# Layer 0 of a two-layer vision Mamba: one x_proj product per chunk for both scan directions, with the kinds of states chosen anew for each half image

## The chip, the core and the metric

The kernel is one program on one core of a Trainium2 chip. The time is device microseconds (us) of one execution. Its engines are named as in the profile: PE (TensorE matrix products), PEld (the loading of TensorE's weights), DVE (VectorE), ACT (ScalarE), POOL (GpSimd) and SP (SyncE, which here issues nearly all DMAs). All data is float32.

## What is computed

The input has 8 images of 48 x 48 positions and 192 channels. Two layers follow each other, each with a residual. The change is in layer 0 alone, whose core is a selective scan over 384 inner channels with 16 states each, run in four directions:

```
xs    = stack([rows, columns, flip(rows), flip(columns)])     # u in four orders, k = 0..3
x_dbl = einsum('bkdl,kcd->bkcl', xs, x_proj_w)                # 12 dt rows, 16 B rows, 16 C rows
dt    = softplus(dt_w @ x_dbl[:12] + dt_bias)
h     = exp(dt*A) * h + (dt*u) * B                            # per step, channel and state
y     = sum over states of h * C
```

Directions 2 and 3 read the same u as 0 and 1, backwards. So x_dbl of direction 2 at a position is another matrix times the same column of u as x_dbl of direction 0. After the scan the four directions are summed, normalised, gated and projected to 192 channels. Layer 1 has two stages of bidirectional Mamba over lines; it keeps its instructions.

## The kernel before

**Tiling.** An *item* is one image, one direction and one chunk of 384 positions (8 rows or columns of 48). An image has 4 x 6 = 24 items, layer 0 has 192, and they run in the order of image, direction, chunk; two neighbours form a *pair*. An item has 16 states, a state has 3 blocks of 128 channels: 48 *segments* of 128 x 384 for each item, 9216 in layer 0. I call items of directions 0 and 1 the forward half of an image and those of 2 and 3 the backward half.

**What a segment costs.** ACT computes `exp(dt*A)` (tile `a`, L515). PE puts `dt*u*B` into one of three PSUM tiles `b`, and DVE runs the scan over both (L1290), which starts from `carry` where the chunk isn't the first. POOL multiplies a state's three blocks by C (tile `g`, L703, one instruction for each state), with C fetched over all partitions from DRAM by a DMA (`cc`, L472). PE adds the product into PSUM (`y`, L720).

**Kinds of states.** How `dt*u*B` is made is written by hand as a letter for each of the 16 states, in `WAYS[0]` (two rows for even and odd items). With kinds `a` and `b` the transposed `dt*u` (`dtu`) is multiplied by B, position by position, and PE transposes the result back: three transposes for each segment (L645). The multiplication is three ACT instructions (`bT`, L553) or one POOL instruction (L543): POOL may take a state only if it is a `b`, ACT may take either, and the planner says which. With kind `m` a diagonal matrix of B is made (`db`: three small ACT instructions, L597, or one of POOL, L594), and PE multiplies `dtu` by it (L639); a float32 product of this kind passes through PE twice, a transpose once. Two further rows hold for the last image, where no next image is being prepared.

**The x_proj step** (`project`, L330). For each item PE multiplies u by `xp` (three products, L350), ACT or DVE copies 44 rows into `xd`, SP stores the B and C rows to DRAM (`bc`, L368), PE transposes `xd` (L380) and ACT or DVE copies the transposed rows into `bt`, which kinds `a`, `b` and `m` read. Then `softplus` multiplies `xd` by `dtw` (L414) and ACT applies the function (L419). The bias of dt is a row of ones in `xd` at row `ONE`.

**What sets the order.** Each engine runs its instructions in program order. That order comes from a planner in the kernel (`Plan.run`): every step is a `Need` with a due time (a segment number plus an offset from `ORDER[0]`), a cost on each engine that may do it, and the steps it needs; the planner simulates the engines and gives each one the step with the lowest due time among those that are ready. `near` is how long past the earliest ready step another one may begin and still be chosen. Two PSUM banks are shared by all small products. A step marked `exps` waits for the planner's leave while ACT's softplus table is loaded.

Of the kernel before, what the change touches and what calls it, by code (L numbers as in the profile page):

```python
# [26 lines left out]
N = 16  # L27
R = 12
E = R + 2 * N
ONE = 64  # L30
RT = 8
T = RT * S
NC = L // T
# [4 lines left out]


WAYS = (  # L40
    ("aabbbbbabbbbbmab", "bbbbbbbabbbbbmab", "ambbmbbbbmbmabbm", "ababbbbmbbabbmba"),
    ("bbbbbbbbbbbdabbb", "bbbdbbbbbmbbabbb", "bbbbbbbbbbbdabbb", "bbbdbbbbbmbbabbb"),
)
PE, DVE, ACT, POOL, SP = "PE", "DVE", "ACT", "POOL", "SP"

# [16 lines left out]

ORDER = (
    dict(
        du=-40, turn=-31, fetch=4, exp=-4, weigh=-5, late_act=1.5, late_pool=1.5, matrix=-5, row=-2,
        wide=-7, there=8.5, zero=-0.5, multiply=-4, broad=-3.5, place=-8.5, carry=7.5, gather=1.5, add=6,
        leave=7, back=6, evac=-5, lo0=-40, mid0=-54, hi0=-42, lo1=-43, mid1=-43, hi1=-52, lead=0, apart=10,
        pro0=8, pro1=-140, pro2=220, tail0=3, tail1=6, near=0,
    ),
    dict(  # L70
        du=-16, turn=-13, fetch=-6, exp=-2, weigh=-3, late_act=1.5, late_pool=-2, matrix=-22.5, row=-24,
# [25 lines left out]
class Need(Mark):  # L97
# [2 lines left out]

    def __init__(self, due, costs, after=(), bank=False, frees=None, sets=(), lag=0.0, late={}, exps=False):
        Mark.__init__(self)
        self.exps = exps
        self.due, self.costs, self.after, self.wants = due, costs, list(after), bank
        self.late = late
        self.frees, self.sets, self.lag, self.bank = frees, sets, lag, None
# [14 lines left out]
class Plan:  # L123
# [4 lines left out]
    def __init__(self):  # L128
        self.clear = dict.fromkeys((PE, DVE, ACT, POOL, SP), 0.0)
        self.lanes = []  # L130
        self.banks = [Mark(0.0, PE), Mark(0.0, PE)]
        self.marks = {}
        self.at = -10**6
        self.exps = True
        self.near = 0.02

    def mark(self, *key):
# [21 lines left out]
        return need  # L159

    def ready(self, need, e):
        if need.exps and not self.exps:
            return None
        after = need.after
        while after and after[-1].t is None:
            return None
        t = 0.0
        for m in after:
            if m.t is None:
                after.remove(m)  # L170
                after.append(m)
                return None
            t = max(t, m.t + (0.0 if m.e == e else LAG[m.e][e]))
        if need.wants:
# [54 lines left out]
class Common:  # L229
# [100 lines left out]
    def project(self, plan, pool, p, pair, lo, mid, hi, which=(0, 1)):  # L330

        nc, mark = self.nc, plan.mark
        tiles = self.tiles.setdefault(p, {})
        gots = []
        for i in which:
            item = pair[i]  # L340
            g, wts = 2 * p + i, item["wts"]
            turned = item.get("turned")
# [11 lines left out]
            xd = self.xds[i]  # L354
            got = Need(at(), COPY, [n] + self.xd_used[i], frees=k)
            yield got
            if turned:
                self.copy(
                    got.e, xd[:E].rearrange("p (w h) -> p w h", h=S),
                    ps[:E, :T].rearrange("p (h w) -> p w h", w=RT),  # L360
                )
            else:
                self.copy(got.e, xd[:E], ps[:E, :T])

            def send(e, i=i, xd=xd):
# [3 lines left out]
                pair[i]["bc"] = tiles["bc"][i]  # L369

            after = [got] + ([mark("cc", g - 5, N - 1)] if g >= 6 else [])
            sent = Need(at(), {SP: 0.1}, after, lag=DMA, sets=[mark("bc", g)])
            yield sent
            send(SP)
            after = [got] + ([mark("place", (g - 2 - i) * NSEG - 1)] if g >= 4 else [])
            n = Need(at(), {PE: 0.33}, after, bank=True)
# [6 lines left out]
            n = Need(at(), {ACT: 0.16, DVE: 0.19}, [n], frees=k, sets=[mark("bt", g)])  # L383
            yield n
            if i == 0:
                tiles["bt"] = pool.tile([P, 2, TB, E], F32, tag="bt", name="bt", bufs=2)
            bt = tiles["bt"]
            item["bt"] = bt[:, i]
            self.copy(n.e, bt[:, i], ps[:, :T].rearrange("p (b e) -> p b e", e=P)[:, :, :E])
            self.xd_used[i] = [n, sent]  # L390
            gots.append(got)
        return gots

    def softplus(self, plan, pool, p, pair, due, after, which=(0, 1)):
# [29 lines left out]
        return ends  # L424

    def opens(self, plan, due, after, opened):
        yield Need(due, {ACT: TABLE}, after, sets=[opened])
        plan.exps = False

    def closes(self, plan):  # L430
# [44 lines left out]
    def stream(self, plan, pool, items, ways, decay, scan, finish, held, kept, weighed, fetched, first=None):  # L475
# [12 lines left out]
        total = len(items) * NSEG  # L488
        das, bts, ccs, bps, hs, gs = {}, {}, {}, {}, {}, {}
        self.xd_used, self.tiles = [[], []], {}  # L490
        way = lambda i, n: ways[2 * (i >= len(items) - 4 * NC) + i % 2][n]
        having = self.having = lambda i, some: [n for n in range(N) if way(i, n) in some]
        K = self.order

# [295 lines left out]
def layer0(ctx, cm, x, xs, x2, w, norm):  # L790
# [355 lines left out]
    def tails():  # L1146
# [4 lines left out]
        for b in range(NIMG):  # L1151
            st = None
            for c in range(NC - 1, -1, -1):
# [19 lines left out]
                for j in range(NJ):  # L1173
                    n = Need(at(), {ACT: 0.42}, [ready] + used[-1:])
                    yield n
                    sq = pool.tile([P, T], F32, tag="sq", name="sq", bufs=1)
                    nc.scalar.activation(sq, a[:, j, :], AF.Square)
                    n = Need(at(), {PE: MM}, [n], bank=(j == 0))
                    yield n
                    used.append(n)  # L1180
                    if j == 0:
                        ps, k = cm.bank(n, "var_ps"), n.bank
                    nc.tensor.matmul(ps[:, :T], ones, sq, start=(j == 0), stop=(j == NJ - 1))
                n = Need(at(), {ACT: 0.9}, [n], exps=True)
                yield n
# [2 lines left out]
                nc.scalar.activation(rs, rs, AF.Exp, scale=-0.5)  # L1188
                n = Need(at(), {DVE: 1.35}, [n], frees=k)
                yield n  # L1190
                nc.vector.tensor_tensor(a, a, rs.unsqueeze(1).to_broadcast((P, NJ, T)), ALU.mult)
                for j in range(NJ):
                    n = Need(at(), {ACT: 0.6}, [n])
# [67 lines left out]
    items, ys = [], {}  # L1261
    for b in range(NIMG):
        for k in range(4):
            rev = k >= 2
            order = range(NC - 1, -1, -1) if rev else range(NC)
            for n, c in enumerate(order):
                item = dict(
                    b=b, k=k, c=c, reverse=rev, carried=(n > 0), A=A[:, k],
                    wts=dict(xp=xp[:, k], dtw=dtw[:, k, :]),
                    u=lambda j, k=k, c=c: by_rows(seen(u, j, k, c), k), turned=k % 2,  # L1270
                    all=seen(u, slice(None), k, c),
                    ready=ready(b, k, c),
                    cost=(MM, 3.1 if k % 2 else 2.6, 0.915),
                    wanted=lambda j, b=b, k=k, c=c: wanted(b, k, c),
                )
                item["softened"] = [mark("dt", len(items))]
                if k < 2:
# [43 lines left out]
def layer1(ctx, cm, x2, xw, dst, w, norm):  # L1321
# [230 lines left out]
    def output(p):  # L1552
# [39 lines left out]
        nc.sync.dma_start((dst if stage else xw)[b][:, :, cs], o)  # L1592

    items = [
        dict(cost=(MM, 2.6, 0.855), sooner=0 if i else SOON, wanted=lambda j, i=i: [mark("silu z", i)]) for i in range(2 * pairs)
    ]

    def first(ps):
# [22 lines left out]
def laid_out(a):  # L1621
# [31 lines left out]
    t["w0_xp"] = widened(np.moveaxis(inner(g("x_proj_w")), 2, 3))  # L1653
# [37 lines left out]
```

## Time and profile before

| | us |
|---|---|
| three runs | 19351.8, 19359.31, 19360.32 (median 19359.31) |
| the profiled execution | 19360.51 |
| its span, which the trace covers | 19358.8 |
| layer 0 in the span (to the first instruction of layer 1) | 0 to about 9704 |

Cut at the first scan of each half image, layer 0 falls into halves of 718.6 and 622.0 us for image 0, of 584.6 to 588.8 (forward) and 608.9 to 614.6 (backward) for images 1 to 6, and of 563.8 and 582.9 for image 7.

The page counts an engine as busy while it runs an instruction, and neighbours on ACT and PE overlap: the mean duration of one is longer than its pitch, the time from its start to the start of the next. Costs are therefore taken from pitches. The timeline prints runs of equal instructions with a start, a length and a number, from which a pitch can be read. The view of stretches gives the busy time of each engine between two times.

### The profile page before, as it was taken

Reading aid. Unit: us, or ns where it says so; the run is one execution under the profiler, and the core shown is the slowest. Engines: PE = TensorE matmul, PEld = TensorE weight load, DVE = VectorE, ACT = ScalarE, POOL = GpSimd, SP = SyncE. Lnnn points to the kernel's source line nnn. Section 1 sums busy time; section 2 is a strip of 40 time slices with the busy share of each in tenths; the row PEclk is TensorE's granted clock in tenths of the full one; section 3 lists DMA queues with packets and bytes.
Section 4 is the critical chain, followed back from the end, with each engine's and each line's share of the span. In section 5 each row is a group of like instructions: output and inputs, shape, how many; then the busy total and the mean of one; then the engine's idle time right before and its main releaser. Section 6 shows DMA issues by size and latency. Waiting matters only on the chain.

```text
span 19358.8 us, 400059 instructions
## 1 busy us (share of the span) xinstructions
PE 18941.4 (98%) x137182; PEld 15944.7 (82%) x137182; DVE 18648.0 (96%) x23348; ACT 19012.3 (98%) x37123; POOL 18799.2 (97%) x8817
## 2 busy tenths in 40 slices
PE   9999999999999999999999999999999999999999
PEld 7888888888888888888878888888888888888887
DVE  8999999999999999999989999999999999999999
ACT  8999999999999999999999999999999999999999
POOL 7999999999999999999989999999999999999999
PEclk9999999999999999999999999999999999999999
DMA  3333333333333333333322222222222222222222
GB/s 91 95 104 95 98 103 94 106 93 99 100 93 108 92 106 97 91 96 85 90 70 72 71 72 70 71 71 71 71 76 72 74 74 74 74 75 74 74 74 71
DMA packets 1572608, 1640.56 MB, mean 85 GB/s; under 512 B 602000, under 2 KB 1536144, under 8 KB 1570448
## 3 DMA queue, kind: packets, MB, share of 16 engines
q1 hardware_dynamic: 1560592, 1588.75, 30.0%
q8 instruction: 1093, 17.91, 0.4%
q10 hardware_dynamic: 9984, 26.21, 0.4%
q14 instruction: 939, 7.69, 0.1%
HBM read 1439.32 MB, written 171.05 MB: 83 GB/s over the span
## 4 chain that ended last, share of the span: by engine, by line
PE 39%; ACT 6%; DVE 3%; issue 1%; POOL 1%; DMA 0%; POOLq 0%; DVEq 0%; ACTq 0%; SPq 0%
PE y L720 12%; PE b L645 11%; PE o_ps L1575 3%; PE xi_ps L1423 3%; PE z_ps L1477 3%; ACT l_da L515 2%; DVE h L1536 2%; ACT bT L553 2%; PE dt_ps L414 2%; PE xd_ps L350 1%; POOL g L703 1%; PE b L639 1%; PE du_ps L457 1%; PE yb_ps L778 1%; PE bb_ps L659 0%
## 5 line engine op out<-in xcount | busy, mean ns | idle before, releaser
L703 POOL TENSOR_TENSOR g<-h,cc 128x1152 f32<-128x1152 f32 x6144 | 14127.6, 2339 | 366.7 <-DVE h L1290 79.4
L645 PE MATMUL b<-ident,bT 128*128 128x128 f32 x50436 | 7997.3, 274 | 146.1 <-DVE h L1290 92.7
L1536 DVE TENSOR_TENSOR_SCAN h<-l_da,b 128x384 f32<-128x384 f32 x9216 | 8061.0, 932 | 67.8 <-PE b L645 44.1
L720 PE MATMUL y<-ident,g 128*128 128x128 f32 x55296 | 7995.4, 273 | 110.3 <-POOL g L703 88.0
L645 PEld LDWEIGHTS b<-ident,bT 128*128 128x128 f32 x50436 | 6079.7, 141 | 2124.3 <-issue 991.1
L1290 DVE TENSOR_TENSOR_SCAN h<-a,carry,b 128x384 f32<-128x384 f32 x7680 | 7081.0, 991 | 296.5 <-ACT a L515 147.7
L553 ACT ACTIVATE bT<-dtu,bt 128x384 f32<-128x384 f32 x11949 | 6941.3, 613 | 10.5 <-PE b L645 8.2
L720 PEld LDWEIGHTS y<-ident,g 128*128 128x128 f32 x55296 | 6403.4, 141 | 482.4 <-POOL g L703 234.6
L515 ACT ACTIVATE a<-dt,l_A 128x384 f32<-128x384 f32 x9216 | 5180.4, 611 | 60.6 <-DVE h L1290 45.3
L515 ACT ACTIVATE l_da<-dt,l_A 128x376 f32<-128x376 f32 x9216 | 5045.0, 605 | 15.9 <-DVE h L1536 12.8
L543 POOL TENSOR_TENSOR bT<-dtu,bt 128x1152 f32<-128x1152 f32 x1621 | 3450.6, 2130 | 57.8 <-PE b L645 37.1
L1290 DVE TENSOR_TENSOR_SCAN h<-a,b 128x384 f32<-128x384 f32 x1536 | 1340.7, 934 | 38.9 <-PE b L645 14.2
L446 POOL TENSOR_TENSOR du<-dt,u 128x1152 f32<-128x1152 f32 x384 | 1082.0, 2818 | 79.6 <-ACT dt L419 79.6
L966 PE MATMUL cv_ps<-pad,diag 128*128 128x384 f32 x2376 | 950.7, 487 | 0.0
L414 PE MATMUL dt_ps<-xd,l_dtw 128*128 128x384 f32 x2304 | 899.2, 496 | 39.8 <-ACT dt L419 27.9
L1575 PE MATMUL o_ps<-z,l_out 128*96 128x384 f32 x2304 | 918.0, 486 | 0.4 <-DVE b L627 0.3
L1477 PE MATMUL z_ps<-xt,l_z 96*128 96x384 f32 x2304 | 916.5, 489 | 2.0 <-DVE u L1452 1.9
L1423 PE MATMUL xi_ps<-xt,l_u 96*128 96x384 f32 x2304 | 907.9, 490 | 9.5 <-ACT xt L1406 6.6
L350 PE MATMUL xd_ps<-u,l_xp 128*128 128x384 f32 x2304 | 895.5, 487 | 1.9 <-ACT bt L273 0.7
L639 PE MATMUL b<-db,dtu 128*128 128x128 f32 x6264 | 829.4, 277 | 5.7 <-DVE h L1290 2.3
L639 PEld LDWEIGHTS b<-db,dtu 128*128 128x128 f32 x6264 | 772.5, 192 | 53.4 <-DVE h L1290 7.5
L1452 DVE SCALAR_TENSOR_TENSOR u<-xi_ps,l_conv_w,u 128x376 f32<-128x376 f32 (+1 forms) x1152 | 665.9, 581 | 24.9 <-ACT u L1442 17.8
(132 smaller groups left out, 12673.8 us busy)
## 6 DMA issues: line engine op xcount, KB each, us to landing
cc<-bc SPq DMA_DIRECT2D x6144, 192.0 KB, 3.1
y<-yt SPq DMA_DIRECT2D x96, 576.0 KB, 3.4
yo<-y SPq DMA_DIRECT2D x96, 576.0 KB, 4.1
xc<-in_x SPq DMA_DIRECT2D x174, 288.0 KB, 4.2
carry<-h SPq DMA_DIRECT2D x2560, 1.5 KB, 2.3
z<-v SPq DMA_DIRECT2D x144, 192.0 KB, 3.3
z<-z SPq DMA_DIRECT2D x48, 576.0 KB, 5.2
v<-v SPq DMA_DIRECT2D x126, 192.0 KB, 2.7
```

The lines of the kernel that those rows point to most:

```text
L515: nc.scalar.activation(dst, src, AF.Exp, scale=item["A"][:, j, n : n + 1])
L543: nc.gpsimd.tensor_tensor(to, of, by.to_broadcast((P, TB, DI)), ALU.mult)
L553: nc.scalar.activation(to[:, b, :], of[:, b, :], AF.Copy, scale=by[:, b, :])
L639: nc.tensor.matmul(ps[:, b * P : (b + 1) * P], item["dtu"][:, b, j * P : (j + 1) * P], dbs[i, n][:, b, :], start=True, stop=True,)
L645: nc.tensor.transpose(ps[:, b * P : (b + 1) * P], of, self.ident)
L703: nc.gpsimd.tensor_tensor(to.rearrange("p j t -> p t j"), h, c, ALU.mult)
L720: nc.tensor.matmul(item["sum"][b][:, j * P : (j + 1) * P], gs[f][:, j, b * P : (b + 1) * P], self.ident, is_transpose=True, skip_group_che ...
L1290: nc.vector.tensor_tensor_scan(order(h[:, :, at % NJ]), order(a), order(b), carry[:, at : at + 1] if item["carried"] else 0.0, ALU.mult, A ...
L1423: nc.tensor.matmul(pieces(ps), wu[d][0][:, m, j * P : (j + 1) * P], lines(xt, m, d), start=(m == 0), stop=(m == NM - 1),)
L1477: nc.tensor.matmul(pieces(ps), wz[d][0][:, m, j * P : (j + 1) * P], lines(xts[p % 3], m, d), start=(m == 0), stop=(m == NM - 1),)
L1536: nc.vector.tensor_tensor_scan(h[:, :, at % NJ], a, b, 0.0, ALU.mult, ALU.add)
L1575: nc.tensor.matmul(ps[:CP, :T], wout[:, 2 * stage + e, j, m * CP : (m + 1) * CP], items[2 * p + e]["z"][:, j, :], start=(e == 0 and j == 0 ...
```

## The change

It has four parts, all in layer 0 but for unused branches:

- `xp` holds for each of the two orders the rows of both directions, 88 in all. An item of directions 0 and 1 computes and copies all 88, transposes them, and stores them to DRAM twice: as they are (all 88 rows, `part`) and transposed (the backward direction's 44, `turn`).
- An item of directions 2 and 3 has no x_proj product, no copy and no transposes: SP loads its 12 dt rows into `xd` and its transposed rows into `bt`. Its C rows are fetched from the stored `part`. The row of ones moves from 64 to 96, so that 88 rows fit.
- `WAYS[0]` has three pairs of rows: forward, backward, last image. The forward rows are those of before; a backward row has three `m` where it had one, and the last image's rows are placed otherwise.
- In `ORDER[0]` some offsets differ (`mid0` -54 to -58, `carry` 7.5 to 6, `fetch` 4 to 3, `near` 0 to 0.02 and others), and two flags keep ACT's softplus table from being loaded between the tail's sum of squares and the exponential that needs it, and the reverse.

```diff
-ONE = 64
+ONE = 96
 WAYS = (
-    ("aabbbbbabbbbbmab", "bbbbbbbabbbbbmab", "ambbmbbbbmbmabbm", "ababbbbmbbabbmba"),
+    ("aabbbbbabbbbbmab", "bbbbbbbabbbbbmab", "abmbbbbabmbbbmab", "bmbbbbbabmbbbmab", "abmbmbbbbmbmbbam", "bbaabbbmbbabbmba"),
...
-        du=-40, turn=-31, fetch=4, exp=-4, weigh=-5, late_act=1.5, late_pool=1.5, matrix=-5, row=-2,
-        wide=-7, there=8.5, zero=-0.5, multiply=-4, broad=-3.5, place=-8.5, carry=7.5, gather=1.5, add=6,
-        leave=7, back=6, evac=-5, lo0=-40, mid0=-54, hi0=-42, lo1=-43, mid1=-43, hi1=-52, lead=0, apart=10,
-        pro0=8, pro1=-140, pro2=220, tail0=3, tail1=6, near=0,
+        du=-40, turn=-31, fetch=3, exp=-4, weigh=-5, late_act=1.5, late_pool=1.5, matrix=-5, row=-4,
+        wide=-6, there=8, zero=-2, multiply=-4, broad=-6.5, place=-8.5, carry=6, gather=1.5, add=6,
+        leave=7, back=6, evac=-4, lo0=-40, mid0=-58, hi0=-42, lo1=-45, mid1=-41, hi1=-52, lead=0, apart=10,
+        pro0=8, pro1=-140, pro2=210, tail0=3, tail1=6, near=0.02,
...
# project(), for each item of a pair
+            bt = tiles["bt"][:, i]
+            item["bt"] = bt[:, :, :E]
+            free = [mark("place", (g - 2 - i) * NSEG - 1)] if g >= 4 else []
+            if "other" in item:
+                got = Need(lo, {SP: 0.2}, self.xd_used[i] + free + [mark("kept", item["other"])], lag=DMA, sets=[mark("bt", g), mark("bc", g)])
+                yield got
+                part, turn = item["saved"]
+                nc.sync.dma_start(xd[:R], part[E : E + R, :])
+                nc.sync.dma_start(bt[:, :, :E], turn)
+                item["bc"] = part[E + R : 2 * E, :]
+                self.xd_used[i] = []
+                gots.append(got)
+                continue
...
-                self.copy(got.e, xd[:E], ps[:E, :T])
+                self.copy(got.e, xd[:e], ps[:e, :T])
...
+            if "saved" in item:
+                part, turn = item["saved"]
+                nc.sync.dma_start(part, xd[:e, :])
+                item["bc"] = part[R:E, :]
...
+            cost = {ACT: 0.16, DVE: 0.19} if e == E else {ACT: 0.27, DVE: 0.33}
...
+            if "saved" in item:
+                n = Need(at(), {SP: 0.1}, [n, sent], lag=DMA, sets=[mark("kept", g)])
+                yield n
+                nc.sync.dma_start(turn, bt[:, :, E:])
# stream()
-        way = lambda i, n: ways[2 * (i >= len(items) - 4 * NC) + i % 2][n]
+        way = lambda i, n: ways[2 * items[i]["kind"] + i % 2][n]
# the two flags
+        if (need.exps and not self.exps) or (need.calm and self.fragile):
-        yield Need(due, {ACT: TABLE}, after, sets=[opened])
+        yield Need(due, {ACT: TABLE}, after, sets=[opened], calm=True)
-                    n = Need(at(), {PE: MM}, [n], bank=(j == 0))
+                    n = Need(at(), {PE: MM}, [n], bank=(j == 0), exps=(j == 0))
# layer0(), for each item
-                    wts=dict(xp=xp[:, k], dtw=dtw[:, k, :]),
+                    wts=dict(xp=xp[:, k % 2], dtw=dtw[:, k, :]), rows=2 * E, kind=2 if b == NIMG - 1 else k // 2,
+                if k < 2:
+                    part = cm.dram.tile([2 * E, T], F32, name=f"xd{b}_{k}_{c}")
+                    turn = cm.dram.tile([P, TB, E], F32, name=f"bt{b}_{k}_{c}")
+                    item["saved"] = saved[b, k, c] = part, turn
+                else:
+                    item["other"], item["saved"] = b * per + (k - 2) * NC + c, saved[b, k - 2, c]
```

More of the change, by code (lines that the diff above doesn't have):

```diff
@@ L40 @@
 WAYS = (
-    ("aabbbbbabbbbbmab", "bbbbbbbabbbbbmab", "ambbmbbbbmbmabbm", "ababbbbmbbabbmba"),
-    ("bbbbbbbbbbbdabbb", "bbbdbbbbbmbbabbb", "bbbbbbbbbbbdabbb", "bbbdbbbbbmbbabbb"),
+    ("aabbbbbabbbbbmab", "bbbbbbbabbbbbmab", "abmbbbbabmbbbmab", "bmbbbbbabmbbbmab", "abmbmbbbbmbmbbam", "bbaabbbmbbabbmba"),
+    ("bbbbbbbbbbbdabbb", "bbbdbbbbbmbbabbb"),
 )
@@ L97, with __init__ @@
 class Need(Mark):
-    def __init__(self, due, costs, after=(), bank=False, frees=None, sets=(), lag=0.0, late={}, exps=False):
+    def __init__(self, due, costs, after=(), bank=False, frees=None, sets=(), lag=0.0, late={}, exps=False, calm=False):
         Mark.__init__(self)
-        self.exps = exps
+        self.exps, self.calm = exps, calm
         self.due, self.costs, self.after, self.wants = due, costs, list(after), bank
@@ L133, in __init__ @@
         self.at = -10**6
-        self.exps = True
+        self.exps, self.fragile = True, 0
         self.near = 0.02
@@ L161, in ready @@
     def ready(self, need, e):
-        if need.exps and not self.exps:
+        if (need.exps and not self.exps) or (need.calm and self.fragile):
             return None
@@ L341, in project @@
             g, wts = 2 * p + i, item["wts"]
+            xd = self.xds[i]
+            if i == 0:
+                tiles["bt"] = pool.tile([P, 2, TB, item["rows"]], F32, tag="bt", name="bt", bufs=2)
+            bt = tiles["bt"][:, i]
[11 more added lines that the diff above has]
+                continue
             turned = item.get("turned")
@@ L353, in project @@
                 )
-            xd = self.xds[i]
+            e = item["rows"]
             got = Need(at(), COPY, [n] + self.xd_used[i], frees=k)
@@ L358, in project @@
                 self.copy(
-                    got.e, xd[:E].rearrange("p (w h) -> p w h", h=S),
-                    ps[:E, :T].rearrange("p (h w) -> p w h", w=RT),
-                )
-            else:
-                self.copy(got.e, xd[:E], ps[:E, :T])
-            def send(e, i=i, xd=xd):
+                    got.e, xd[:e].rearrange("p (w h) -> p w h", h=S),
+                    ps[:e, :T].rearrange("p (h w) -> p w h", w=RT),
+                )
+            else:
+                self.copy(got.e, xd[:e], ps[:e, :T])
+            after = [got]
+            if "saved" not in item:
+                after += [mark("cc", g - 5, N - 1)] if g >= 6 else []
+            sent = Need(at(), {SP: 0.1}, after, lag=DMA, sets=[mark("bc", g)])
+            yield sent
+            if "saved" in item:
[3 more added lines that the diff above has]
+            else:
                 if i == 0:
@@ L368, in send @@
                 nc.sync.dma_start(tiles["bc"][i], xd[R:E, :])
[L369 to L376, printed above, removed]
+                item["bc"] = tiles["bc"][i]
+            n = Need(at(), {PE: 0.33}, [got] + free, bank=True)
             yield n
@@ L382, in project @@
                 )
-            n = Need(at(), {ACT: 0.16, DVE: 0.19}, [n], frees=k, sets=[mark("bt", g)])
+            cost = {ACT: 0.16, DVE: 0.19} if e == E else {ACT: 0.27, DVE: 0.33}
+            n = Need(at(), cost, [n], frees=k, sets=[mark("bt", g)])
             yield n
[L385 to L389, printed above, removed]
+            self.copy(n.e, bt, ps[:, :T].rearrange("p (b e) -> p b e", e=P)[:, :, :e])
             self.xd_used[i] = [n, sent]
             gots.append(got)
+            if "saved" in item:
+                n = Need(at(), {SP: 0.1}, [n, sent], lag=DMA, sets=[mark("kept", g)])
+                yield n
+                nc.sync.dma_start(turn, bt[:, :, E:])
         return gots
@@ L1182, in tails @@
                         ps, k = cm.bank(n, "var_ps"), n.bank
+                        plan.fragile += 1
                     nc.tensor.matmul(ps[:, :T], ones, sq, start=(j == 0), stop=(j == NJ - 1))
@@ L1190, in tails @@
                 yield n
+                plan.fragile -= 1
                 nc.vector.tensor_tensor(a, a, rs.unsqueeze(1).to_broadcast((P, NJ, T)), ALU.mult)
@@ L1259, in put_carry @@
         nc.sync.dma_start(carry[:, q * NJ : (q + 1) * NJ], h[:, 0 if rev else T - 1, :])
-    items, ys = [], {}
+    items, ys, saved = [], {}, {}
     for b in range(NIMG):
@@ L1276, in layer0 @@
                 item["softened"] = [mark("dt", len(items))]
+                if k < 2:
+                    part = cm.dram.tile([2 * E, T], F32, name=f"xd{b}_{k}_{c}")
+                    turn = cm.dram.tile([P, TB, E], F32, name=f"bt{b}_{k}_{c}")
+                    item["saved"] = saved[b, k, c] = part, turn
+                else:
+                    item["other"], item["saved"] = b * per + (k - 2) * NC + c, saved[b, k - 2, c]
                 if k < 2:
@@ L1594, in layer1 @@
     items = [
-        dict(cost=(MM, 2.6, 0.855), sooner=0 if i else SOON, wanted=lambda j, i=i: [mark("silu z", i)]) for i in range(2 * pairs)
+        dict(cost=(MM, 2.6, 0.855), rows=E, kind=0, sooner=0 if i else SOON, wanted=lambda j, i=i: [mark("silu z", i)]) for i in range(2 * pairs)
     ]
@@ L1652, in laid_out @@
     t["w0_conv_b"] = inner(g("conv_b"))
-    t["w0_xp"] = widened(np.moveaxis(inner(g("x_proj_w")), 2, 3))
+    v = np.moveaxis(inner(g("x_proj_w")), 2, 3)
+    t["w0_xp"] = widened(np.concatenate([v[:, :2], v[:, 2:]], -1))
     t["w0_dtw"] = with_bias(g("dt_w"), g("dt_bias"))
```

## Prediction

> **What bounds layer 0.** The change touches layer 0 alone, so I first cut the span there and read the busy times of one image's two halves, forward and then backward (time; busy us and instructions of PE, PEld, DVE, ACT, POOL; clock, DMA share, GB/s).
>
> ```profile
> core 0: us, PE busy (x) PEld busy (x) DVE busy (x) ACT busy (x) POOL busy (x), PEclk, DMA share, GB/s
> 3732.00:4320.00 588.00, 576.08 (x4227) 490.52 (x4226) 553.56 (x646) 581.12 (x1147) 580.70 (x284) 1.00 0.34 95
> 4320.00:4930.00 610.00, 586.04 (x4334) 498.92 (x4333) 579.76 (x682) 602.93 (x1177) 589.47 (x285) 1.00 0.39 103
> ```
>
> ACT is busy 98.8% in both halves. POOL is level with it in the forward half and has 3% to spare in the backward one; DVE has 5 to 6%. The halves of the other images from 1 to 6 last as long within 5 us. In images 1 to 7 (1340 to 9673 us) ACT is busy 8236 of 8333 us: 97 us idle. The waits of that stretch say who waits for whom (us, times, longest):
>
> ```profile
> ACT pad L956 <- PE xi_ps L915: 23.6, 21, 4.0
> ACT v L280 <- PE xi_ps L915: 15.3, 17, 5.4
> ...
> DVE h L1290 <- ACT a L515: 133.0, 76, 5.1
> DVE h L1290 <- issue: 39.8, 59, 2.5
> DVE h L1290 <- PE b L645: 37.5, 92, 1.8
> ```
>
> DVE's largest wait is for ACT; ACT's own waits are small and spread. So ACT's work sets the pace, and a gain must be ACT time that goes away, or some of those 97 us.
>
> **Pitches.** Instructions overlap with the next, so I price by the time from start to start, from the timeline at 4400 us (start, length, what, how many):
>
> ```profile
> 4400.07 1.00 ACT L597 ACTIVATE db<-ident,bt 128x128 f32<-128x128 f32 x3
> ...
> 4400.95 2.15 ACT L515 ACTIVATE a<-dt,l_A 128x384 f32<-128x384 f32 x4
> ...
> 4405.34 0.74 PEld L639 LDWEIGHTS b<-db,dtu 128*128 128x128 f32 x6 [0.16 <-DVE h L1290]
> ...
> 4408.15 0.36 PEld L645 LDWEIGHTS b<-ident,bT 128*128 128x128 f32 x3
> ...
> 4419.65 1.23 ACT L273 COPY yt<-y 128x384 f32<-128x384 f32 x3
> ```
>
> One `a` lasts 0.61 us, so four in 2.15 have a pitch of (2.15 - 0.61)/3 = 0.51; `bT` has the same shape and gets 0.51. Three `db` take from 4400.07 to the next start at 4400.95: 0.88. A copy of 384 columns lasts 0.48, so (1.23 - 0.48)/2 = 0.37. On PE a pass of 128 columns takes 0.11 ((0.36 - 0.14)/2), a product of kind m two of them, and a pass of 384 columns 0.325 (starts of neighbouring `xd_ps` rows). On POOL a `bT` takes 2.07 and a `db` 0.80, on DVE a copy 0.46 (starts again).
>
> **The counts.** I set the instructions of both programs against each other, engine by engine. Outside layer 0's rows below nothing changes in number; table loads stay at 602.
>
> *ACT.* `bT` 11949 to 11670: -279 x 0.51 = -142.3. `db` 384 to 807: +423 x 0.293 = +123.9. `xd` copies 265 to 190 (width in time is 384 columns whether 44 or 88 rows): -75 x 0.37 = -27.8. `bt` copies of 132 columns 264 to 143: -121 x 0.15 (their start-to-start time) = -18.2; 57 new ones of 264 columns: the trace has none, so between 0.15 and 0.37, taken at 0.26, half way as their width is: +14.8 (bounds +8.6 and +21.1). Other copies and biased copies that the planner now gives to ACT: 16 x 0.37 + 15 x 0.46 = +12.8. Sum **-36.7 us**, bounds -43 to -30.
>
> *POOL.* `bT` -75 x 2.07 = -155.3, `db` +27 x 0.80 = +21.6: **-134**. *DVE.* Fewer copies: **-25**. *PE.* 288 x_proj products less: -288 x 0.65 = -187; 288 transposes less: -32; 1512 transposes become products: 1512 x 0.11 = +166: **-53**.
>
> So the shared product itself saves ACT little (copies, about -31 us); its point is the PE time, which pays for more `m` states, and those spare ACT 3 x 0.51 = 1.53 for 0.88.
>
> **Where it lies.** The same sums for each half image, cut at each engine's own 576th step:
>
> | us | ACT | POOL | DVE | PE |
> |---|---|---|---|---|
> | image 0 | +6.7 | -29.9 | -6.9 | -3.9 |
> | images 1 to 6, forward halves | +2.2 | +21.3 | -4.7 | -0.4 |
> | images 1 to 6, backward halves | -38.0 | -125.5 | -11.9 | -19.2 |
> | image 7 | -7.6 | +0.5 | -1.4 | -29.0 |
>
> In the backward halves ACT's saving (6.3 each) is on the path: ACT stays the fullest engine (604 of about 605, POOL 567, DVE 582, PE 567 in pitches). POOL's 21 us per half become idle time, worth nothing beyond ACT's. Forward halves: nothing. Image 0: its +7.5 on ACT falls into the first half, where ACT is idle 12%; I count 0 (bounds 0 and +7.5). Sum: +2.2 - 38.0 - 7.6 = -43.4. Against the profiled execution (19360.5): 19317; the median of the runs lies 1.2 lower, so **19316**, 0.22% less than before.
>
> **The moved and added waits.** Each backward item adds two loads on SP, each forward item one more store: 192 DMAs more among some 6,300 of layer 0, at 0.3 to 0.6 us of issue; SP needs about 0.8 us of issue in a state of 2.8. Nothing shows these loads; the nearest rows are the `xd` store (48 KB, median 2.3 us, 1.5 to 7.0) and the `y` load (576 KB, 4.1). They are due 40 segments, some 38 us, before their item, so they are hidden: 0. Without that cover, 48 pairs x 2.3 to 7.0 would cost 110 to 336; below nothing, the first `cc` fetch of a backward item need no longer wait for a fresh store, at most the 1.6 us that POOL waits for `cc` in the stretch. The load waits for `xd` and `bt` to be free; behind it on SP stand `cc` fetches and carries. A `cc` fetch runs up to four states (11 us) ahead of its use and lands in 3.2, so some 8 us of delay are free; a `carry` store is needed an item later. The two flags hold back a PE step or a table load in the planner; in the trace no softplus falls between a tail's first square sum and its exponential (48 of 48), so I count 0.
>
> Smaller pieces have a rule against them. The Trainium skill (DMA: Bandwidth & Descriptors, Specifications) asks for at least 512 bytes a piece and says that smaller ones are read, modified and written back. The transposed store and load go in pieces of 176 bytes. But the `carry` store goes in pieces of 4 bytes, and landed after 2.6 us in the median and 8.7 at most in one backward half. By the rule these loads would be slower, by the row they land within the 38 us; the sum is the same.
>
> **Where the order could take it back.** The planner made a new order with other offsets, so the 97 us of idle time are not kept by right; that is the main uncertainty. What the order itself shows is calm: in forward halves a segment is placed on PE 8.0 segments (mean) ahead of the additions, before it was 8.2; in backward halves 9.1 against 8.5. Image 7 of before already runs with some 43 `m` states in each half, and there ACT is busy 561.7 of 564 and 574.2 of 582: more `m` has not made ACT wait.
>
> **Rivals.**
>
> *The forward halves pay.* POOL's load rises 2 to 5 us in each forward half of images 1 to 6, by 21.3 in all, and POOL is as busy there as ACT. If POOL sets the pace there, 21 less 2 already counted goes: 19316 + 19 = **19335**. For: 580.7 of 588 busy. Against: part of it is only the cut, since one `du` step moves from the backward half across it, and POOL's backward half has room.
>
> *Idle time goes as well.* With POOL 5% emptier in backward halves and fewer small products on PE, ACT may wait less. Half of the 97 us: 19316 - 48 = **19268**. For: ACT's waits are for PE products. Against: PE's load in the forward halves, where most of those products lie, stays.
>
> *PE cannot place the `m` segments in time; slower.* A state of kind m needs 3 x (0.74 + 0.36) = 3.3 us of PE with its additions by the timeline, its three scans 3 x 0.93 = 2.8; three PSUM tiles allow two scans of lead. With 168 more such states, each stalled by s, the gain is gone at s = 43/168 = 0.26 us, and slower by over 0.2% needs 0.49. At 0.5 us: 19316 + 84 = **19400**. Against: the scans waited 4.6 us in all for the 228 such states of images 1 to 7, 0.02 each. For: in images 1 to 6 PE is fuller than in image 7. In passes it has 564 us of work in a forward half of 587 and 570 in a backward one of 610.
>
> How full PE is, the skill reads otherwise. It (Perfetto Trace Analysis, Identifying the Most-Contended Engine) discards PE's busy share and takes that of weight loading: 490.5 of 588 here, 83%. By the passes above it is 96%. By the rule this rival would have no chance and the sum would stand; by the rows it keeps one.
>
> *It does not do what it says.* Excluded by count: 1152 x_proj products become 864.
>
> **Numbers.** Chances: forecast (19298 to 19330) 0.46, forward halves pay or the idle time grows a little (19331 to 19380) 0.24, idle time goes as well 0.16, slower rival 0.14. About 0.2% (39 us) is what a measurement of this kernel can tell from no change: the marks are 19321 and 19398. Of the forecast's case some two thirds lie below 19321: 0.31, with 0.16 makes faster 0.47; slower takes 0.13 of the last rival; the rest, 0.40, is the same. The range leaves out the deepest part of the idle case and half of the slower one: 19262 to 19392.
>
> **What would show it.** Right: backward halves of images 1 to 6 last 603 to 607 us, forward ones 586 to 590; ACT stays at 98.5 to 99%; POOL falls to 94% in backward halves; no wait for the `bt` or `xd` loads; layer 1 within 3 us. Wrong: scans waiting for products of kind m well over 0.1 us for each such state, ACT below 98%, forward halves over 592, or layer 1 moved.

## The result, and the profile after

The changed kernel takes **19391.39 us** (median of 17 runs, 19380.89 to 19398.28), the kernel before 19355.75 in the same measurement (17 runs, 19347.9 to 19360.32): a ratio of 1.0018, 95% interval 1.0011 to 1.0024. It is 36 us slower; 43 us less were forecast. The profiled execution of after took 19380.89 (span 19379.2), at the low end of its runs, that of before 19360.51 (span 19358.8), at the high end. So the traces hold 20.4 of the 36 us, and the account by place below goes by spans.

Cut at the first scan of each half image, the difference of the two spans lies here:

| us | forecast | measured |
|---|---|---|
| image 0 | 0 | +12.4 |
| images 1 to 6, forward halves | +2.2 | +2.3 |
| images 1 to 6, backward halves | -38.0 | **+10.8** |
| image 7 | -7.6 | -4.5 |
| layer 1 | 0 | -0.6 |
| sum | -43.4 | +20.4 |

Of the 63.8 us between the two sums, 48.8 are in the backward halves of images 1 to 6 and 12.4 in image 0. The view of stretches for image 3's two halves in after (time; busy us and instructions of PE, PEld, DVE, ACT, POOL; clock, DMA share, GB/s), the halves that the prediction shows of before:

```profile
core 0: us, PE busy (x) PEld busy (x) DVE busy (x) ACT busy (x) POOL busy (x), PEclk, DMA share, GB/s
3754.80:4341.40 586.60, 574.91 (x4215) 487.30 (x4213) 550.38 (x642) 582.47 (x1149) 580.58 (x284) 1.00 0.37 98
4341.40:4952.60 611.20, 587.01 (x4459) 511.35 (x4460) 580.34 (x679) 595.19 (x1179) 573.63 (x279) 0.99 0.38 104
```

In the backward half ACT's busy time fell from 602.9 to 595.2 and POOL's from 589.5 to 573.6: the work left, as counted. The half still lasts 611 us. ACT is idle 16 us of it, where it was idle 7. Over images 1 to 6 as one stretch, first before and then after, the same view says:

```profile
1340.50:8526.70 7186.20, 6975.07 (x51382) 5940.57 (x51380) 6797.37 (x7953) 7099.41 (x13925) 7027.92 (x3402) 1.00 0.36 98
```

```profile
1353.00:8552.30 7199.30, 6979.13 (x52036) 5996.76 (x52034) 6780.48 (x7895) 7067.75 (x13959) 6925.38 (x3362) 1.00 0.38 100
```

ACT was spared 31.7 us (7099.4 to 7067.8; the count for these images was 35.8). Its **idle time grew from 86.8 to 131.6 us**, by 44.8. All of the growth is in the backward halves: summed over the six images, ACT's idle time goes from 49.2 to 103.3 us there, and from 37.6 to 28.2 in the forward halves. The view of waits of the stretch from 1340 to 9650 us names what ended that idle time in after (waiter, releaser; us, times, longest):

```profile
ACT a L535 <- DMA cc<-xd: 20.2, 2, 10.5
ACT a L535 <- DMA u<-v: 18.8, 2, 9.5
ACT a L535 <- DVE h L1318: 15.3, 29, 6.0
ACT yt L273 <- PE y L740: 14.9, 5, 5.8
...
ACT a L535 <- DMA carry<-h: 8.6, 1, 8.6
```

Three releasers here are DMAs, and their five waits last 47.6 us, some 9 us each. In before the same view has one such line:

```profile
ACT a L515 <- DMA carry<-h: 6.6, 1, 6.6
```

An exponential `a` doesn't read `u`, `cc` or the store of `carry`. So the name of the releaser is a label that needs a look: what stands ahead of that `a` in ACT's program order? The timeline of ACT at the end of image 3 in after, the kernel's own line L1107:

```profile
4869.37 0.53 ACTq L1107 DMA_DIRECT2D u<-v  x1
4869.50 0.60 ACT L573 ACTIVATE bT<-dtu,bt 128x384 f32<-128x384 f32 x1
4870.01 0.60 ACT L535 ACTIVATE a<-dt,l_A 128x384 f32<-128x384 f32 x1
4870.43 9.65 ACTq L1107 DMA_DIRECT2D u<-v  x2
4880.13 0.61 ACT L535 ACTIVATE a<-dt,l_A 128x384 f32<-128x384 f32 x1 [9.52 <-DMA u<-v]
```

and of before (L1087):

```profile
4840.47 0.53 ACTq L1087 DMA_DIRECT2D u<-v  x1
4841.04 0.84 ACTq L1087 DMA_DIRECT2D u<-v  x1
4841.30 0.64 ACT L515 ACTIVATE a<-dt,l_A 128x384 f32<-128x384 f32 x1
4841.91 0.63 ACTq L1087 DMA_DIRECT2D u<-v  x1
4843.02 0.60 ACT L515 ACTIVATE a<-dt,l_A 128x384 f32<-128x384 f32 x1
```

Here ACT itself issues DMAs: three loads of 1152 KB each that bring the next image's `u`, issued by `enters()` two items before the image begins. Before, all three go out within 1.5 us. After, the third goes out 9.1 us behind the second, and ACT stands behind it. The gaps ahead of the third load at the end of images 1 to 6 are 7.7, 8.3, 8.6, 9.0, 8.6 and 4.6 us: 46.9 in all, about the size of the new idle time. In before the same place costs 5.5 us, all of it at the end of image 6. A seventh gap, of 8.6 us, stands at the end of image 0 (3.1 in before).

**Why the third load waits.** Each DMA of layer 0 is counted by one of eight semaphores (100 to 107), taken in turn in program order. In every program here a DMA is issued only once the one eight places earlier, which holds its semaphore, has landed. The landing events of the trace, after (start of the issue, issuer, what, semaphore, us to the last landing):

```
4869.37 ACT u<-v      100   8.03
4870.43 ACT u<-v      103  10.32
4872.00 SP  carry<-h  106   7.49     <- landed at 4879.49
4872.56 SP  cc<-xd    107   8.38
4879.56 ACT u<-v      106   6.08
```

The three loads stand at places n, n+3 and n+6 of the order of DMAs; before they stood at n, n+3 and n+4. Semaphore 106 was last taken by a `carry` store that SP issued *after* the first two loads. That store is 1.5 KB and otherwise lands in 2 to 3 us; behind two large loads it took 7.5. So ACT waits for a small store that is slow behind ACT's own loads. At the end of image 0 the third load's semaphore is still held by the first load itself. Before, the third load's semaphore was last taken by a `carry` issued at 4836.47, which landed at 4840.83, ahead of the load.

### The profile page after: what moved, and what is told of

The parts are those of the page before. It is cut to its first block, busy times and chain, and to the rows that moved or that the text cites. A ratio compares the mean times of both kernels' runs of the same rounds, so it can differ in the third digit from the quotient of the medians.

```text
span 19379.2 us, 401618 instructions
## 1 busy us (share of the span) xinstructions
PE 18930.5 (98%) x137830; PEld 15998.6 (83%) x137830; DVE 18624.3 (96%) x23264; ACT 18980.6 (98%) x37159; POOL 18667.9 (96%) x8769
## 4 chain that ended last, share of the span: by engine, by line
PE 61%; ACT 17%; DVE 4%; POOL 2%; issue 2%; DMA 1%; DVEq 0%; POOLq 0%; SPq 0%; ACTq 0%
PE y L740 19%; PE b L665 18%; ACT a L535 6%; ACT bT L573 5%; PE o_ps L1603 3%; PE xi_ps L1451 3%; PE z_ps L1505 3%; PE b L659 3%; PE dt_ps L434 2%; PE cv_ps L986 2%; POOL g L723 2%; DVE h L1564 2%; PE xd_ps L366 2%; ACT l_da L535 2%; PE du_ps L477 1%
## 5 line engine op out<-in xcount | busy, mean ns | idle before, releaser
L665 PE MATMUL b<-ident,bT 128*128 128x128 f32 x48924 | 7759.8, 274 | 161.9 <-DVE h L1318 85.5
L665 PEld LDWEIGHTS b<-ident,bT 128*128 128x128 f32 x48924 | 5879.0, 141 | 2037.9 <-issue 917.3
L573 ACT ACTIVATE bT<-dtu,bt 128x384 f32<-128x384 f32 x11670 | 6786.0, 613 | 21.5 <-PE b L665 19.4
L563 POOL TENSOR_TENSOR bT<-dtu,bt 128x1152 f32<-128x1152 f32 x1546 | 3280.2, 2123 | 58.4 <-PE b L665 34.4
L659 PE MATMUL b<-db,dtu 128*128 128x128 f32 x9288 | 1239.1, 277 | 5.4 <-DVE h L1318 4.6
L659 PEld LDWEIGHTS b<-db,dtu 128*128 128x128 f32 x9288 | 1150.6, 192 | 77.2 <-DVE h L1318 12.0
L366 PE MATMUL xd_ps<-u,l_xp 128*128 128x384 f32 x1728 | 668.0, 487 | 0.9 <-issue 0.5
```

Source lines behind the costliest of these rows:

```text
L563: nc.gpsimd.tensor_tensor(to, of, by.to_broadcast((P, TB, DI)), ALU.mult)
L573: nc.scalar.activation(to[:, b, :], of[:, b, :], AF.Copy, scale=by[:, b, :])
L659: nc.tensor.matmul(ps[:, b * P : (b + 1) * P], item["dtu"][:, b, j * P : (j + 1) * P], dbs[i, n][:, b, :], start=True, stop=True,)
L665: nc.tensor.transpose(ps[:, b * P : (b + 1) * P], of, self.ident)
```

## The experiments

Two kinds of kernels were tried: those that alter the loads of `u`, and those that separate the four parts of the change.

**One large load instead of three**, in after and in before.

```diff
-                    for i in range(3):
-                        part = slice(i * L // 3, (i + 1) * L // 3)
-                        nc.scalar.dma_start(u[:, :, part], vs[b][:, :, part])
+                    nc.scalar.dma_start(u, vs[b])
```

> The changed kernel with one edit: ACT fetches the next image's u with one DMA where it issued three. Theory A (the third of the three loads must wait for a small transfer of SP that stands behind the first two, and ACT waits with it, 4.6 to 9.5 us at each of seven image changes, 56 us in all): those gaps go, the time falls by 40 to 60 us, to 19330 to 19350. Theory B (the other offsets in the order cost the time): it stays at 19385 to 19400. Theory C (more states of kind m than PE can place in time): it stays as well.

Measured: 19384.49 (19378.72 to 19388.31, 11 runs), ratio to before 1.0013, interval 1.0004 to 1.0021. The gain expected did not come. ACT no longer waits for its own load, but:

```profile
ACT a L535 <- DVE h L1316: 46.7, 52, 7.6
```

In this view of ACT's waits (1353 to 9000 us) the idle time has moved to the scan: at the end of image 3 one load of 3.4 MB holds up the `carry` and `cc` transfers for 7 to 12 us, the scans wait for them, and `a`'s buffers don't come free.

> The kernel before with the same edit, one DMA for u. Theory A: the kernel before has only two gaps of some 4 us at its loads (images 1 and 7), so it gains 3 to 12 us, to 19344 to 19353. Theories B and C: no change, within 5 us of 19356. With the first run of this call it gives the change's worth without the stall: by theory A the changed kernel should then be faster than the kernel before, by the 36.7 us of ACT work that was counted, give or take 20.

Measured: 19390.69 (19378.79 to 19396.02, 11 runs), 1.0016, interval 1.0007 to 1.0025. The expectation missed in sign: the kernel before, changed at this one line, becomes as slow as after, with some 45 us of gaps at this place. So this place alone can cost what the change lost. With one load in both, after is 6 us the faster, and not by the 17 to 57 us expected.

**The offsets alone.** `ORDER[0]` of before in after, and of after in before; nothing else.

> The changed kernel with the offsets (ORDER[0]) of the kernel before, all else as changed. Theory B: the loss goes and the counted saving shows, 19316 to 19340. Theory A: the time follows the gaps at the three u loads in its own trace: with gaps as in the changed kernel 19380 to 19400, without them 19330 to 19350. Theory C: 19385 to 19400.

Measured: 19397.95 (19390.97 to 19411.38, 11 runs), 1.0022, interval 1.0013 to 1.0031. The gaps at the loads of `u` remain: 37 us over the seven image changes, where after has 55.5 (the time that ACT stands still ahead of a load, gaps over 1 us).

> The kernel before with the offsets of the changed one, nothing else. Theory B: slower, 19390 to 19430, since it has the offsets' loss and not the saving. Theory A: slower by as much as its trace shows in gaps at the u loads, 0 to 56 us. Theory C: no change, 19350 to 19362.

Measured: 19353.64 (19349.48 to 19360.67, 11 runs), 0.9997, interval 0.9989 to 1.0006: no difference, but of two that cancel. The gaps at the loads of `u` are 32 us, against 9 of before, and the kernel is faster in other places: by the traces the forward halves of images 1 to 6 are 13 us shorter, the backward ones, which hold most of the gaps, 1 us, and image 0 is 7 us longer. Theory B, that the new offsets are what costs, falls. Theory C expected this time and that of the run before as well; it is answered by the runs without loads. So the offsets alone and the other parts alone (the run before this one) each bring gaps at the loads of `u`.

A further run, e8, is this same kernel once more. Gaps of 4.8 to 5.8 us at six image changes and forward halves of 582 to 588 us were expected; it gave 19359.46 in one execution, with six gaps of 4.7 to 6.1 us and forward halves of 581.6 to 587.6.

**No loads of `u` at all**, in after and in before. Images 1 to 7 use image 0's `u`; the three lines are left out.

> The changed kernel without the loads of u for images 1 to 7: every image is scanned with what stands in u from image 0, the rest is as it was. Left out: 21 DMAs of 1152 KB. Theory A (the loss is the stall at these loads, and the counted saving on ACT is there elsewhere): 19325 to 19345, at least 45 us less than the changed kernel, and 0 to 40 us less than the kernel before without its loads. Theory D (the shared product or the kinds lose the time in all of the backward half): at most 20 us less than the changed kernel, and still slower than the kernel before without its loads.

> The kernel before without the same 21 loads (images 1 to 7 use image 0's u). Theory A: it loses only some 10 us of gaps, 19340 to 19355. Theory D: the same.

Measured: after 19332.5 (19325.79 to 19337.9, 11 runs; 0.9987, interval 0.9978 to 0.9996), before 19342.8 (19328.7 to 19354.13, 11 runs; 0.9991, interval 0.9982 to 1.0000). The loads cost after 59 us and before 15 (19391.4 - 19332.5; 19358 - 19342.8). The engines do the same work in the same halves as with the loads: ACT's instruction counts by half agree to one instruction. The 44 us between the two costs settle the first half of the miss; theories B and C had no place for them, and theory D allowed after 20 us at most. The second half is also seen: without the loads the change is worth 10 us and not 43. The spread of the runs leaves 3 to 17 us for these 10, and the two traces differ by 3.4. By spans its backward halves of images 1 to 6 gain 23, its forward halves pay 12, image 0 pays 11.5.

**The three loads apart**, all work done: three steps with 12 segments between them.

```diff
-                    n = Need(lo - 10, {ACT: 0.3}, [mark("du", g - 1), mark("v", b)] + used, lag=9.0)
-                    yield n
                     for i in range(3):
+                        n = Need(lo - 36 + 12 * i, {ACT: 0.1}, [mark("du", g - 1), mark("v", b)] + used, lag=4.0)
+                        yield n
                         part = slice(i * L // 3, (i + 1) * L // 3)
```

> The changed kernel with the three loads of u as three steps, due 12 segments apart from 36 segments ahead of the pair's first step, in place of one step. In the order that results they stand 10 and 11 DMAs apart for images 3 and 4, and 4 apart for images 2, 5 and 6. Each DMA waits for the one eight places before it. Theory A: images 3 and 4 lose their gap (the item with the loads 6 to 9 us shorter), those with loads 4 apart keep a wait, since the third then waits for the first to land; in all 10 to 40 us less than the changed kernel. Theory D: no change, 19385 to 19400.

Measured: 19345.28 (19341.6 to 19352.5, 11 runs), 0.9994, interval 0.9985 to 1.0003: 46 us below after, a little more than expected. Of the gaps at this place 9.6 and 5.4 us are left at the loads for images 1 and 2, and 1.5 to 2.9 at three others; images 3 and 4 have none.

**The parts, without the loads.** The next three leave out the 21 loads, so that the stall can't hide anything. The first is before with after's offsets, the corner; the second adds the new kinds (`WAYS[0]`) to it; the third is the shared product with the kinds of before. The two flags for the softplus table are in the code of after alone, so they go with the shared product in all of these runs and were not tried apart.

> The kernel before with the offsets of after, and without the 21 loads of u (images 1 to 7 read image 0's u): no shared product, kinds as before. It is the corner from which the two next runs differ by one part each. Theory D (the new offsets are worth some 25 us outside the stalls at the u loads, and the shared product with the new kinds then gives about 14 of them back): 19342.8 - 25 = 19318, between 19310 and 19326. Theory E (the offsets are worth nothing once no load is in the way, and the small gain of after without loads comes from the shared product and the kinds): 19336 to 19350.

Measured: 19306.37 (19303.42 to 19310.96, 8 runs), 0.9974, interval 0.9964 to 0.9983. Against before without loads the offsets alone give **36 us**, more than theory D's 25 (28 us between the two traces, which lie 11 us in the forward and 23 in the backward halves of images 1 to 6, with image 0 8 us longer).

> The run above with the kinds of states of after (backward halves and last image), still one x_proj product for each item, and without the loads of u. Some 480 ACT multiplications become 423 diagonals: by the counts ACT is spared 18 us against the corner, PE gets 168 more states of three products, and keeps its 288 x_proj products. Theory D with the kinds as the culprit: 8 to 20 us slower than the corner. Theory D with the shared product as the culprit, and theory E: 5 to 20 us faster than the corner, in the backward halves.

Measured: 19383.77 (19378.58 to 19391.67, 10 runs), 1.0015, interval 1.0005 to 1.0024: 77 us above the corner.

> The kernel after with the kinds of before in all halves, without the loads of u: the shared product alone. By the counts ACT is spared 31 us of copies against the corner and PE some 220. Theory D with the shared product as the culprit (88-row copies, stores and loads on SP, x_proj work moved into the forward halves): 8 to 20 us slower than the corner, forward halves 587 to 591 and image 0 longer by 8 or more. With the kinds as the culprit: at or below the corner in the backward halves, 5 to 20 us faster in all.

Measured: 19418.23 (19413.6 to 19426.01, 5 runs), 1.0033, interval 1.0020 to 1.0045: 112 us above the corner. No theory had sizes like these, and they don't add: both parts together (the run of after without loads) are 26 above the corner, not 189. In the third, ACT waits for one product before the copies of `y` in four images:

```profile
ACT yt L273 <- PE y L740: 55.3, 10, 9.7
```

A part taken alone makes another order, with stalls of its own: the longest, 9.7 us, stands at the same place of images 2 to 5 and is not in after. So the two kernels do not price the parts, and the pair of theories about which of them is the culprit stays open. What can be compared is the corner and after without loads. The corner first, images 1 to 6, then after without loads:

```profile
1342.20:8476.10 7133.90, 6970.93 (x51383) 5933.11 (x51382) 6807.67 (x7977) 7081.95 (x13895) 7034.21 (x3405) 1.00 0.35 96
```

```profile
1345.50:8502.70 7157.20, 6973.32 (x52033) 5999.23 (x52032) 6778.63 (x7894) 7066.35 (x13959) 6924.98 (x3362) 1.00 0.36 98
```

The parts spare ACT 15.6 us and POOL 109, and ACT's idle time rises from 52.0 to 90.9: they cost 23.3 us here. At 52.0 the corner's order is the tightest of all. By halves, summed over the six images: the forward halves are 23.0 us longer, and ACT works 21.4 us more in them (3472.9 to 3494.3) and is idle 1.5 more. Some 10 of the 21.4 are exponentials of the next half that ACT runs earlier; the rest is work that the planner gives to ACT there. In the backward halves ACT works 37.0 us less and is idle 37.3 more (17.5 to 54.8), so nothing is gained. The waits of ACT from 1340 to 9650 us, the corner:

```profile
ACT yt L273 <- PE y L720: 13.4, 6, 10.9
...
ACT bT L553 <- PE b L645: 1.9, 5, 0.5
```

and after without loads:

```profile
ACT yt L273 <- PE y L740: 30.8, 6, 10.7
ACT bT L573 <- PE b L665: 12.6, 26, 1.2
```

Of each first line some 11 us lie at the end of layer 0. In after without loads the other 20 us are five gaps of 3.3, 3.3, 3.7, 6.4 and 3.5 us, all in the third item of a backward half. SP's timeline ahead of the second of them shows what has come there:

```profile
4409.57 0.54 SPq L352 DMA_DIRECT2D xd<-xd  x1
4410.20 0.57 SPq L353 DMA_DIRECT2D bt<-bt  x1
4410.82 0.57 SPq L352 DMA_DIRECT2D xd<-xd  x1
4411.44 0.56 SPq L353 DMA_DIRECT2D bt<-bt  x1
4412.10 0.56 SPq L492 DMA_DIRECT2D cc<-xd  x1
4412.76 0.62 SPq L853 DMA_DIRECT2D xc<-in_x  x1
```

The four added loads of a pair take 2.5 us of SP's issue (4 x 0.62 from start to start), and the load of `xc`, a piece of the next image, stands behind them. PE then waits 2.1 us for `xc` with a product `xi_ps`, the scans wait 2.6 for PE and ACT 3.3 for `y`. All five gaps show the same list on SP, with PE's wait for `xc` at 2.1 to 4.2 us; the corner has none over 1.9. The planner charges 0.2 us for two loads that take 1.24. This is read from the trace. The same five gaps stand in after (14.9 us, the `yt` line of its waits above). A kernel that moves these loads behind `xc` was not run, so it isn't shown that the 20 us would come back. One run speaks against it: after with its loads apart issues the same four loads and has none of these five gaps, and still ACT is idle 68.5 us in its backward halves, some 12 of them at the loads of `u`; there `bT` waits 17 us for PE and `a` 13 us for the scans. So what keeps ACT idle in the backward halves is not settled.

**The best version.** Before with after's offsets and the loads apart: no shared product, kinds as before, all work done.

> The kernel before with two edits: the offsets of after, and the three loads of u as three steps 12 segments apart. No shared product, kinds as before; all work is done. If the offsets are worth 25 us outside the stalls and spreading takes the stalls away (as it took 46 us off after): 19322 to 19335, faster than both kernels and than after with spread loads (19345). If the offsets are worth nothing by themselves: 19345 to 19355.

Measured: **19315.45** (19309.56 to 19320.53, 11 runs), 0.9978, interval 0.9969 to 0.9987: 42 us below before, 76 below after, and below the range that was expected. Images 1 to 6:

```profile
1342.40:8482.70 7140.30, 6974.90 (x51383) 5936.60 (x51382) 6810.25 (x7977) 7083.57 (x13895) 7034.59 (x3405) 1.00 0.36 99
```

ACT is idle 56.7 us, 30 less than before, and busy 16 us less. Against the same offsets and spread loads with the shared product and the new kinds (19345.28) it is 30 us faster. By place this looks like the 26 us of the corner (the forward halves differ by 23.2 us here and by 23.0 there), but it is no second measurement of them: that kernel still has 22 us of gaps at the loads of `u`, and this one has none.

## Why the prediction was wrong

By medians the runs lead from one kernel to the other: before 19357.6; without loads -14.8; offsets -36.4; shared product, kinds and flags +26.1; the loads again, at after's order, +58.9; after 19391.4. The terms are differences of neighbouring runs, so their sum closes by itself; the spread of the runs leaves each of them some 4 to 8 us either way, and before itself had medians from 19355.8 to 19359.6 in the four measurements.

*What bounds the kernel.* Right: ACT's busy time is 98 to 99% wherever it isn't stalled, and before and after differ by ACT's idle time: its work fell, and the span grew.

*The counts.* Right in size. Images 1 to 6 lost 31.7 us of ACT where 35.8 were counted, and 102.5 of POOL where 104 were. But half of it does not belong to the parts named: with the new offsets alone the planner already gives ACT 16 us less (7083.6 in the best version), and the shared product, the kinds and the flags spare it the other 16 (15.6 from the corner to after without loads).

*Where it lies.* This is the step that failed: "In the backward halves ACT's saving (6.3 each) is on the path". It was on the path in most items: summed over images 1 to 6, items 12 to 21 of an image are 49.4 us shorter in after, and items 22 and 23, where the loads of `u` stand, are 60.2 longer. That makes the +10.8 of the table, where -38.0 were forecast.

*The moved and added waits.* The terms set to 0 are what went wrong, in one way that the runs show and in one that is read from a trace. I asked what the added DMAs wait for and who waits for their data, and counted SP's issue. I did not ask what else shares the DMAs' order. ACT issues three loads in each image, and a new order of the DMAs shifts their places (the offsets alone did it, and so did the other parts alone). In after the third waits for a `carry` behind the first two: 46.9 us of gaps in images 1 to 6, where before has 5.5. The added loads on SP were called hidden, since their data has 38 us of cover. It has: no wait for them is in the trace of after. The queue behind them hasn't, and at five places an `xc` load is late behind them.

*"The 97 us of idle time are not kept by right"* was the right warning, with half its sign: I gave a chance to a gain there and priced the loss at the scans of kind `m` alone. The offsets alone made the largest gain of all (36 us), which I had not costed by itself.

*The rivals.* Of the slower rival the end came (about 19391 to 19400) and not the mechanism: the scans waited 19.0 us for the products of kind `m` in after, 39 times, for some 396 such states of images 1 to 7: 0.05 us each, far from 0.49 (the view of waits from 1340 to 9694 us):

```profile
DVE h L1318 <- PE b L659: 19.0, 39, 1.1
```

"The forward halves pay" is right in its size between the corner and after without loads (23 us by spans; 21 were priced for POOL), and not for its reason: ACT's own work grew by 21.4 us there and its idle time by 1.5, so ACT hardly waited more for POOL or for anything else; between before and after the offsets hide it (+2.3). "Idle time goes as well" is what the offsets do without the other parts.

*The signs named.* Backward halves at 610 to 616 instead of 603 to 607 and ACT at 97% there said that it was wrong; POOL at 94% there, forward halves at 585.5 to 589.3 and layer 1 within 0.6 us were as forecast.

*Image 0* was costed at 0 and pays 12.4. The loads don't explain it, since it pays 11.5 without them as well. By the corners 8 of these come with the offsets and 3 with the parts; which wait it is stays open.

## What to carry to other kernels

When a change adds or moves DMAs, list every engine that issues transfers, not only the queue that is changed: where completion semaphores are shared in turn, a busy engine can wait for an unrelated small store. Price an added DMA twice, by the cover of its data and by the issue time that it puts ahead of the next transfer on its queue, with the measured 0.62 us and not the planner's number. (What the second price cost here is read from a trace and not tried.) In an order that a planner makes anew, set the saved busy time against the idle time of the engine that sets the pace; here, in six images, 32 us of work went and 45 us of waiting came.

## What the runs showed of the hardware

- Behind large loads that ACT issues, small transfers that SP issues are slow: `carry` stores of 1.5 KB land in 1.6 to 5.3 us (median 2.8) in before from 4700 to 4830 us, and in 2.2 to 8.7 (median 6.8) from 4838 to 4853, beside the three loads of 1152 KB; beside one load of 3.4 MB up to 12 at the end of image 3 and up to 14 elsewhere.
- A DMA whose semaphore is still in use holds the issuing engine, not only its queue: 9.1 us pass on ACT from the second load to the third, and the exponential behind it in program order, which reads none of the loaded data, starts only then.
- At each of the seven stalls of after PE stands idle too, for 4.1 to 6.0 us, and the granted clock is 0.5 for 6.8 to 10.2 us. In before the clock dips beside one of the seven loads alone, for 6.8 us, at the end of image 6, where ACT was held as well. What the dips add to the time was not measured.
